# Chunk 0 of a two-layer kernel: heads 8 to 15 with the two batches of a pair exchanged on the partitions

## The chip, the cores and the metric

The kernel runs on one core of a Trainium2 chip. Its engines are TensorE (PE, matrix multiplications into the accumulator memory PSUM), VectorE (DVE), ScalarE (ACT), GpSimd (POOL) and SyncE (SP, which here issues transfers). Each engine executes its own instructions in order, and semaphores make one engine wait for another. The metric is the device time of one execution in microseconds: the median over several runs.

## The reference

Two layers, each a token mixer and a feed-forward block on the same normalised input. What the change touches is the second layer's mixer, a test-time-training layer with 16 heads of 64, working through each of 8 sequences of 256 tokens in 4 chunks of K = 64. Cut to the step that is looped over the chunks:

```
xq, xk, xv = hidden @ wq, hidden @ wk, hidden @ wv      # per head, per chunk
def step((W, b), (q, k, v)):
    eta  = token_eta * sigmoid(k @ theta + theta_bias) / HD
    Z1   = k @ W + b
    xhat = (Z1 - mean(Z1)) / std(Z1)
    go   = g * xhat + beta - (v - k)
    grad = (HD*go*g - sum(go*g) - xhat * sum(go*g*xhat)) / (HD * std)
    W    = W - einsum('bhkc,bhkd->bhcd', eta * k, grad)
    b    = b - sum over tokens (eta * grad)
    out  = q + g * normalise(q @ W + b) + beta
    return (W, b), out
```

W and b start the same for every sequence (W1 and b1). The first layer has a gated scan and a ternary feed-forward block with two gelu layers of 512 x 512; the second layer also has a mixture of 8 experts (two per token, chosen by `gate_w`) and a shared expert. All is float32.

## The kernel before, in words

**Tiles.** A tile of 128 partitions holds the 64 tokens of one chunk for two sequences: partitions 0 to 63 are the first batch of the pair, 64 to 127 the second. There are NCH = 4 chunks and NBP = 4 pairs, so the mixer has 16 units u, with chunk n = u // 4 and pair bp = u % 4. `xnT[n]` holds the normalised inputs of chunk n transposed (128 features on the partitions, 128 tokens of a pair along the row).

**One unit.** `keys` and `project_target` call `project` (L912), which multiplies the tokens of a pair with wk or wv: two matmuls, j = 0 for heads 0 to 7 and j = 1 for heads 8 to 15, each 128 tokens x 512, into two PSUM banks. ScalarE copies the keys to `xk`. `keys_T` transposes them (`pxkT`, L928), `apply_keys` multiplies by W (`pz`, L959), `states` adds the bias, `normalise` and `gradient` work out the gradient g on VectorE and GpSimd. `steps_of_W` then makes dW (`pw`, L1123) and the sums over tokens db (`pb`, L1130). `update` subtracts them (`W`, L1142; `B`, L1143), `apply_queries` multiplies the queries by the new W (`pzq`, L959), `outputs` adds B, and the rest normalises, transposes and mixes the heads (`poT`, `po`, L1184 and L1191).

**Quarters of the array.** `pw` and `pz` consist of 64 x 64 matmuls. The input partitions (0 to 63 or 64 to 127) and the output partitions fix which quarter of the 128 x 128 array a matmul uses, and the four orders of (a, b) in the loops use all four. `pb` is made by two full matmuls with `block_ones`, a 128 x 128 matrix with ones in its two diagonal blocks and zeros elsewhere: every batch's tokens are summed and written to all 64 partitions of that batch.

**The order.** Work of three units overlaps: in turn u, unit u computes its states, unit u - 1 its gradient and update, unit u - 2 its output. Between these, a `filler` issues pieces of other work: the first layer's feed-forward block of the following chunks (p, pm, po: L255 to L288), its residual and layernorm (L299, L186 to L202), the gates (L316), the routing, and later the experts. Up to the end of the first layer's scan all engines but GpSimd follow the order in which the program is written. In the mixer VectorE follows it, and TensorE and ScalarE are ordered by a planner.

**Gates.** `gates` (L316) multiplies each pair's tokens with `gw`, 24 columns: 8 for the experts' scores, 16 for the learning rate of each head, from which `eta` follows. The scores lead to the routing: with those of chunk 3 complete, VectorE makes `taken` (L667), SyncE reads values from it, and the experts' weights are fetched.

**PSUM.** Four single banks and two pairs of banks are rotated. `pk`, `pv`, `pxkT`, `pq`, `pz`, `pzq`, `pw`, `pb` and `poT` each take a pair, and wait until the one before it in that pair has been read.

Of the kernel before, what the change touches and what calls it, by code (L numbers as in the profile page):

```python
# [14 lines left out]
ALU = mybir.AluOpType  # L15
# [9 lines left out]
HH = H // 2  # L25
# [3 lines left out]
E = 8  # L29
# [27 lines left out]
C_EW2, C_EB1, C_EB2 = FF, 2 * FF, 2 * FF + 4  # L57
NEW = C_EB2 + D
I32 = mybir.dt.int32

# [11 lines left out]
def tile_two_layers(ctx: ExitStack, tc: tile.TileContext, t: dict, out: bass.AP):  # L74
    nc = tc.nc
# [10 lines left out]
    def bank(name):  # L86
        return ps1.tile([P, 512], F32, tag="bank", name=name)

    def two_banks(name):
        return ps2.tile([P, 2, 512], F32, tag="two", name=name)  # L90

    def resident(name, shape):
        return const.tile(shape, F32, tag=name, name=name)

    def resident_i(name, shape):
        return const.tile(shape, I32, tag=name, name=name)

    def load(name, shape, pool=const):
        sb = pool.tile(shape, F32, tag=name, name=name)
        nc.sync.dma_start(out=sb, in_=t[name])  # L100
        return sb
# [6 lines left out]
    block_ones = resident("block_ones", [P, P])  # L108
# [33 lines left out]
    xnT = [resident(f"xnT_{n}", [P, NBP, P]) for n in range(NCH)]  # L142
# [27 lines left out]
    def later(f):  # L170
        pending.append(f)
# [40 lines left out]
    def empty_rows(pool):  # L212
# [9 lines left out]
    nc.gpsimd.iota(  # L222
        second.bitcast(I32), [[P, NT]], base=B * S, channel_multiplier=1
    )
    nc.gpsimd.tensor_copy(second, second.bitcast(I32))
    wgt = resident("wgt", [P, NT, 2])
# [3 lines left out]
    gw = resident("gw", [P, E + H])  # L230
# [15 lines left out]
    def ffn_steps(n):  # L246

        s = {}
# [56 lines left out]
        def norm():  # L305
            s["row"] = const.tile([P, NBP, ROW], F32, tag="xn1", name="xn1")
            s["xn"] = s["row"][:, :, 0:D]
            ln_apply_T(x1[n], s["stats"], s["xn"], xnT[n])
            nc.gpsimd.tensor_copy(s["row"][:, :, D], second[:, mine])
            nc.gpsimd.tensor_tensor(x1[n], x1[n], kc[:, None, :].to_broadcast([P, NBP, D]), ALU.add)  # L310
            later(gates)

        def gates():
            s["pg"] = bank("pg")[:, : NBP * (E + H)].rearrange("p (b c) -> p b c", b=NBP)
            for bp in range(NBP):
                nc.tensor.matmul(s["pg"][:, bp, :], lhsT=xnT[n][:, bp, :], rhs=gw, start=True, stop=True)  # L316
            later(scores)

        def scores():
# [76 lines left out]
    with (  # L396
# [22 lines left out]
        wk = load("wk", [P, HC])  # L419
# [5 lines left out]
        wv = load("wv", [P, HC])  # L425
# [7 lines left out]
        hp = [l0b.tile([P, B, S + 3], F32, tag="hp", name="hp") for half in range(2)]  # L433
# [84 lines left out]
        for two in range(NBP // 2):  # L518

            pxp = bank("pxp").rearrange("p (b s) -> p b s", b=2)  # L520
            for half in range(2):
                for i in range(2):
                    b = 2 * (2 * two + i)
                    nc.tensor.matmul(
                        pxp[i * 64 : i * 64 + 64], lhsT=xp_w[:, half, :], rhs=hs[half][:, b : b + 2, :],
                        start=(half == 0), stop=(half == 1),
                    )
            part = xpT[:, 2 * two : 2 * two + 2, 0:S]
# [81 lines left out]
        for hp_ in range(HH):  # L610
            nc.tensor.matmul(
                pf2, lhsT=bpad[:, hp_, :], rhs=wo[:, hp_, :], start=(hp_ == 0), stop=(hp_ == HH - 1)
# [28 lines left out]
    def routing_steps():  # L641
        r = {}

        def work(name):

            return side["moe"].tile([P, NEW], F32, tag="ew", name=name, bufs=4)

        def constants():
            r["empty"] = empty_rows(side["moe"])
            w = r["w"] = work("rt_w")  # L650
            ints = w[:, 0:NJ].bitcast(I32)
            nc.gpsimd.iota(ints, [[1, NJ]], base=0, channel_multiplier=0)
# [123 lines left out]
    def routed_tokens_T(g):  # L776
        if g < NG:
            pt = bank("pxg")[:, : GJ * P].rearrange("p (j q) -> p j q", j=GJ)
            src = xg.pop(g)
            for j in range(GJ):  # L780
                nc.tensor.transpose(pt[:, j, :], src[:, j, 0:D], ident)
            ats[g] = side["moe"].tile([P, GJ], I32, tag="ats", name="ats", bufs=3)

# [109 lines left out]
    Wst = [l1.tile([P, 2, HH, HD], F32, tag=f"W_{bp}", name=f"W_{bp}") for bp in range(NBP)]  # L893
    Bst = [l1.tile([P, H, HD], F32, tag=f"B_{bp}", name=f"B_{bp}") for bp in range(NBP)]

    def heads(ap):
        return ap.rearrange("p (h d) -> p h d", h=H)
# [5 lines left out]
    def pairs_of(heads):  # L903
        return slice(heads.start // 2, heads.stop // 2)

    def full(ap):
        return ap.rearrange("p a b -> p (a b)")

    def project(xT, w, name):
        pp = two_banks(name)  # L910
        for j in range(2):
            nc.tensor.matmul(pp[:, j, :], lhsT=xT, rhs=w[:, j * 512 : (j + 1) * 512], start=True, stop=True)  # L912
        return heads(full(pp))

    def transpose_pairs(src, name, bufs=2, heads=ALL, held=None):
# [81 lines left out]
    class Unit:  # L997
# [10 lines left out]

        def keys(self):
            self.xk = l1b.tile([P, H, HD], F32, tag="xk", name="xk", bufs=3)  # L1010
            nc.scalar.copy(self.xk, project(xnT[self.n][:, self.bp, :], wk, "pk"))

        def keys_T(self):
            _, self.xkT = transpose_pairs(self.xk, "xkT", bufs=1)
# [4 lines left out]
                query_pairs(self.u // 2, HH // 2 * (self.u % 2))  # L1019

        def project_target(self):
            self.pv = project(xnT[self.n][:, self.bp, :], wv, "pv")

        def target(self):

# [77 lines left out]
        def steps_of_W(self, k=ALL):  # L1103
            if self.n == NCH - 1:

                part = pairs_of(k)
                for hp in range(part.start, part.stop):
                    for a in range(2):
                        for b in range(2):
                            rb = slice(b * 64, b * 64 + 64)  # L1110
                            nc.tensor.matmul(
                                self.z4[rb, a, hp, :], lhsT=self.at[rb, a, hp, :],
                                rhs=self.g[rb, 2 * hp + a, :], start=False, stop=(hp == HH - 1),
                            )
                return
            g = self.g
            self.pw = two_banks("pw")
            w4 = self.pw.rearrange("p b (h d) -> p b h d", h=HH)
            for hp in range(HH):
                for a in range(2):  # L1120
                    for b in range(2):
                        ra, rb = slice(a * 64, a * 64 + 64), slice(b * 64, b * 64 + 64)
                        nc.tensor.matmul(  # L1123
                            w4[ra, b, hp, :], lhsT=self.xk[rb, 2 * hp + a, :], rhs=g[rb, 2 * hp + a, :],
                            start=True, stop=True,
                        )
            self.w4 = w4
            self.pb = two_banks("pb")
            for j in range(2):
                nc.tensor.matmul(  # L1130
                    self.pb[:, j, :], lhsT=block_ones, rhs=full(g[:, j * HH : (j + 1) * HH, :]),
                    start=True, stop=True,
                )

        def update(self):

            if self.n == NCH - 1:
                return
            W, b = self.old()
            if self.n == 0:  # L1140
                W = W0[:, None].to_broadcast([P, 2, HH, HD])
            nc.vector.tensor_tensor(Wst[self.bp], W, self.w4, ALU.subtract)  # L1142
            nc.vector.tensor_tensor(Bst[self.bp], b, heads(full(self.pb)), ALU.subtract)  # L1143

        def apply_queries(self):
# [79 lines left out]
    for u in range(units - 1):  # L1225
# [3 lines left out]
        z, g, o = live.get(u), live.get(u - 1), live.pop(u - 2, None)  # L1229
# [76 lines left out]
    o, g, z = live[units - 3], live[units - 2], live[units - 1]  # L1306
# [202 lines left out]
```

## Time and profile before

| what | us |
|---|---|
| median of 9 runs | 582.08 (581.05 to 584.19) |
| the profiled execution | 583.11 |
| its span, first to last instruction | 581.4 |
| TensorE busy in the span | 534.7 |
| VectorE busy | 412.8 |
| pk, pv (L912), 64 records each | 31.8 each |
| pb (L1130), 48 records | 24.6 |
| pw (L1123), 768 records | 14.7 |
| pg (L316), 32 records | 5.0 |

A float32 matmul appears as two records in the profile. In a line such as `130.07 1.98 PE L1130 MATMUL pb<-gx,block_ones 128*128 128x512 f32 x4`, the numbers are the start and length in us, then come engine, line, operation, the tile written and the tiles read, the rows and columns of the array in use, the size moved, and the count of records. An idle time before it and what ended it follow in square brackets. In a table by stretch the columns are the stretch, its length, the busy time of TensorE's matmuls, its weight loads, VectorE, ScalarE and GpSimd, then the granted clock of TensorE, the share of the DMA engines and GB/s. The units of chunk 0 make their sums at about 130, 184, 233 and 262 us; their projections lie between 85 and 221 us.

### The profile page before, as it was taken

The page shows a single profiled execution, that of the slowest core. Times are in us where ns is not written, and L with a number is a line of the kernel's source. Part 1 is how long each engine was busy: PE and PEld are TensorE (multiplying, and loading weights), DVE is VectorE, ACT ScalarE, POOL GpSimd, SP SyncE. Part 2 cuts the span into 40 slices and gives each one's busy share as a digit, 9 for nine tenths or more (in the row PEclk, how much of TensorE's full clock was granted, in tenths as well). Part 3 has the DMA queues.
Part 4 walks back from the last instruction along what each step waited for, and adds up shares of the span by engine and source line. Part 5 has one row for each costly group of instructions (what it writes and reads, how often), then busy time and mean ns, then how long its engine had stood idle before and what let it go on. Part 6 is the DMA issues. An engine that isn't in the chain of part 4 may idle for free.

```text
span 581.4 us, 14158 instructions
## 1 busy us (share of the span) xinstructions
PE 534.7 (92%) x5887; PEld 369.9 (64%) x5887; DVE 412.8 (71%) x652; ACT 251.4 (43%) x436; POOL 289.0 (50%) x256
## 2 busy tenths in 40 slices
PE   5999999999999899998968899999999999999655
PEld 2443656465456546576755777888888887878644
DVE  4697353466650585757998598978888777878884
ACT  3655545316420443324505254553635546253246
POOL 6216103751651146542754456576755748467620
PEclk9999999999999799999989899999999999999888
DMA  7900200100000000000015425454353633100302
GB/s 282 406 12 25 61 1 6 33 1 2 12 14 13 1 9 15 17 0 2 19 53 167 141 93 172 135 191 146 108 174 118 203 116 125 43 16 6 109 20 89
DMA packets 25057, 45.89 MB, mean 79 GB/s; under 512 B 3860, under 2 KB 16026, under 8 KB 24481
## 3 DMA queue, kind: packets, MB, share of 16 engines
q1 hardware_dynamic: 22720, 40.75, 21.3%
q0 software_dynamic: 2272, 4.24, 2.2%
q8 instruction: 46, 0.75, 0.5%
q14 instruction: 19, 0.15, 0.1%
HBM read 38.30 MB, written 7.13 MB: 78 GB/s over the span
## 4 chain that ended last, share of the span: by engine, by line
PE 72%; DVE 12%; SPq 5%; issue 3%; ACT 3%; DMA 2%; POOL 2%; DVEq 0%; ACTq 0%; POOLq 0%
PE pm L271 19%; PE phd L804 5%; PE pv L912 4%; PE pyr L819 4%; PE pq L944 4%; PE pk L912 4%; PE po L1191 3%; PE pb L1130 3%; PE p L255 2%; PE po L282 2%; PE pz L959 2%; PE p L257 2%; PE pw L1123 2%; PE py L744 2%; DMA ew<-in_moe_w 2%
## 5 line engine op out<-in xcount | busy, mean ns | idle before, releaser
L271 PE MATMUL pm<-g,h 128*128 128x512 f32 x256 | 113.5, 595 | 0.0
L165 POOL TENSOR_TENSOR rstd<-rs_v,neg_half 128x16 f32<-128x16 f32 x31 | 92.2, 2973 | 2.6
L271 PEld LDWEIGHTS pm<-g,h 128*128 128x128 f32 x256 | 48.1, 190 | 59.8 <-issue 57.5
L1049 POOL TENSOR_TENSOR gx<-xh,gam 128x1024 f32<-128x1024 f32 (+1 forms) x17 | 38.3, 2252 | 81.7 <-DVE er L1048 56.1
L809 ACT ACTIVATE rhid<-phd,ew 128x128 f32<-128x128 f32 x156 | 44.6, 371 | 49.4 <-PE phd L804 38.1
L164 POOL TENSOR_SCALAR rs_v<-var 128x16 f32<-128x16 f32 x31 | 7.7, 247 | 93.4 <-DVE var L987 92.9
L275 ACT ACTIVATE g<-pm,cols 128x512 f32<-128x512 f32 x32 | 22.0, 687 | 68.3 <-PE pm L271 68.2
L804 PE MATMUL phd<-xgT,ew 128*128 128x128 f32 x312 | 43.9, 281 | 1.4 <-DMA ew<-in_moe_w 1.4
L153 POOL DMA_INDIRECT y_dram<-ys,ats x39 | 40.5, 1038 | 9.3 <-issue 9.3
L804 PEld LDWEIGHTS phd<-xgT,ew 128*128 128x128 f32 x312 | 39.4, 192 | 8.6 <-issue 5.1
L987 DVE TENSOR_REDUCE var<-sq 128x16 f32<-128x1024 f32 (+1 forms) x33 | 38.9, 1180 | 8.0 <-ACT sq L981 7.9
L819 PE MATMUL pyr<-ew,rhid 128*128 128x128 f32 x312 | 41.7, 275 | 0.0
L1027 DVE TENSOR_TENSOR u<-rows_b,pv 128x1024 f32<-128x1024 f32 x16 | 19.5, 1219 | 28.2 <-PE pv L912 28.1
L819 PEld LDWEIGHTS pyr<-ew,rhid 128*128 128x128 f32 x312 | 38.5, 192 | 1.5 <-issue 1.4
L1050 POOL TENSOR_TENSOR gx<-gx,u 128x1024 f32<-128x1024 f32 (+1 forms) x17 | 38.2, 2250 | 1.3
L153 POOL DMA_INDIRECT xg_dram<-xn,slot x32 | 34.4, 1076 | 8.3 <-issue 7.4
L981 ACT ACTIVATE sq<-o 128x1024 f32<-128x1024 f32 (+1 forms) x17 | 17.1, 1010 | 46.3 <-DVE o L970 46.3
L1191 PE MATMUL po<-wo,oT 128*128 128x128 f32 x256 | 33.0, 285 | 0.7 <-ACT oT L932 0.7
L912 PE MATMUL pk<-wk,xnT 128*128 128x512 f32 x64 | 31.8, 617 | 0.4 <-DVE o L970 0.4
L1191 PEld LDWEIGHTS po<-wo,oT 128*128 128x128 f32 x256 | 31.5, 201 | 1.0 <-ACT oT L932 0.9
L912 PE MATMUL pv<-wv,xnT 128*128 128x512 f32 x64 | 31.8, 617 | 0.0
L944 PE MATMUL pq<-xnT,wq 128*128 128x256 f32 x128 | 31.1, 383 | 0.4 <-DVE B L1143 0.4
(219 smaller groups left out, 1066.4 us busy)
## 6 DMA issues: line engine op xcount, KB each, us to landing
ew<-in_moe_w SPq DMA_DIRECT2D x39, 578.0 KB, 4.0
xg<-xg_dram SPq DMA_DIRECT2D x39, 65.0 KB, 3.2
h<-in_h SPq DMA_DIRECT2D x2, 1024.0 KB, 9.4
yc<-y_dram SPq DMA_DIRECT2D x8, 256.0 KB, 3.7
x<-in_x SPq DMA_DIRECT2D x4, 256.0 KB, 4.2
rows_g<-in_rows_g SPq DMA_DIRECT2D x1, 1024.0 KB, 7.7
rows_b<-in_rows_b SPq DMA_DIRECT2D x1, 1024.0 KB
w<-in_w SPq DMA_DIRECT2D x3, 256.0 KB, 3.9
```

What stands on the lines that cost most here:

```text
L153: ins = nc.gpsimd.indirect_dma_start(**what).ins
L165: turn[:] = [nc.gpsimd.tensor_tensor(dst, v[:, :width], neg_half[:, :width], ALU.pow).ins]
L271: nc.tensor.matmul(pm, lhsT=w[:, k, m * P : (m + 1) * P], rhs=s[src][:, k, :], start=(k == 0), stop=(k == 3),)
L804: nc.tensor.matmul(ph[:, ms], lhsT=w[:, ms], rhs=xgT[j // GJ][:, j % GJ, :], start=True, stop=True)
L809: nc.scalar.activation(hid[:, m, :], ph[:, ms], AF.Gelu, bias=w[:, C_EB1 + m : C_EB1 + m + 1])
L819: nc.tensor.matmul(py, lhsT=hid[:, m, :], rhs=w[:, C_EW2 + m * D : C_EW2 + (m + 1) * D], start=(m == 0), stop=(m == 3),)
L912: nc.tensor.matmul(pp[:, j, :], lhsT=xT, rhs=w[:, j * 512 : (j + 1) * 512], start=True, stop=True)
L944: nc.tensor.matmul(pq[:, i, :], lhsT=wq[:, (h0 + i) * P : (h0 + i + 1) * P], rhs=xnT[n][:, 2 * half : 2 * half + 2, :], start=True, stop=True,
L987: nc.vector.tensor_reduce(v[:, heads], sq[:, heads], AX.X, ALU.add)
L1049: nc.gpsimd.tensor_tensor(g, xh, gam2[:, k], ALU.mult)
L1050: turn[:] = [nc.gpsimd.tensor_tensor(g, g, self.t[:, k], ALU.add).ins]
L1191: nc.tensor.matmul(self.po, lhsT=self.oT[1][:, hp, :], rhs=wo[:, hp, :], start=False, stop=(hp == HH - 1),)
```

## The change

In chunk 0, heads 8 to 15 of all that is indexed by token have the second batch on partitions 0 to 63 and the first on 64 to 127. W and b are the same for every sequence at this point, so the work in between need not know of it. Three places make the exchange, two undo it:

- `project` with `turned`: the matmul of j = 1 becomes two of 64 columns, each taking the other batch's 64 tokens.
- `gates` for chunk 0: the learning rates of heads 8 to 15 are made in the same way, two matmuls of 64 output partitions and 8 columns, beside one full matmul of 16 columns per pair.
- `steps_of_W` leaves its sums to `sums`: in chunk 0, four matmuls of 64 x 64 on 512 columns take the place of the two with `block_ones` in full. For j = 0 they use the diagonal quarters, for j = 1 the other two, which puts the sums back to their own batch.
- `update` in chunk 0: dW of heads 8 to 15 lies in the other bank, so the subtraction is split into two instructions, the second reading the banks in reverse order.
- `pb` is allocated before the matmuls of `pw`, in all chunks but the last.

```diff
         def gates():
...
-                nc.tensor.matmul(s["pg"][:, bp, :], lhsT=xnT[n][:, bp, :], rhs=gw, start=True, stop=True)
+                xT, pg = xnT[n][:, bp, :], s["pg"][:, bp, :]
+                if n:
+                    nc.tensor.matmul(pg, lhsT=xT, rhs=gw, start=True, stop=True)
+                    continue
+                same = slice(0, E + HH)
+                nc.tensor.matmul(pg[:, same], lhsT=xT, rhs=gw[:, same], start=True, stop=True)
+                for b in range(2):
+                    nc.tensor.matmul(
+                        pg[b * 64 : b * 64 + 64, E + HH :], lhsT=xT[:, 64 - b * 64 : 128 - b * 64],
+                        rhs=gw[:, E + HH :], start=True, stop=True,
+                    )
...
+    def project(xT, w, name, turned=False):
...
+            if turned and j:
+                for b in range(2):
+                    nc.tensor.matmul(
+                        pp[b * 64 : b * 64 + 64, j, :], lhsT=xT[:, 64 - b * 64 : 128 - b * 64], rhs=wj,
+                        start=True, stop=True,
+                    )
+            else:
+                nc.tensor.matmul(pp[:, j, :], lhsT=xT, rhs=wj, start=True, stop=True)
...
+        def sums(self):
+
             for j in range(2):
-                nc.tensor.matmul(
-                    self.pb[:, j, :], lhsT=block_ones, rhs=full(g[:, j * HH : (j + 1) * HH, :]),
-                    start=True, stop=True,
-                )
+                gj = full(self.g[:, j * HH : (j + 1) * HH, :])
+                if self.n:
+                    nc.tensor.matmul(self.pb[:, j, :], lhsT=block_ones, rhs=gj, start=True, stop=True)
+                    continue
+                for b in range(2):
+                    rb, to = slice(b * 64, b * 64 + 64), b if j == 0 else 1 - b
+                    nc.tensor.matmul(
+                        self.pb[to * 64 : to * 64 + 64, j, :], lhsT=block_ones[rb, rb], rhs=gj[rb],
+                        start=True, stop=True,
+                    )
...
-            nc.vector.tensor_tensor(Wst[self.bp], W, self.w4, ALU.subtract)
+                for part, w4 in ((slice(0, HH // 2), self.w4), (slice(HH // 2, HH), self.w4[:, ::-1])):
+                    nc.vector.tensor_tensor(Wst[self.bp][:, :, part], W[:, :, part], w4[:, :, part], ALU.subtract)
+            else:
+                nc.vector.tensor_tensor(Wst[self.bp], W, self.w4, ALU.subtract)
```

`project` is called with `turned` set to `self.n == 0` for the keys and for the targets; the queries are not turned.

More of the change, by code (lines that the diff above doesn't have):

```diff
@@ L907, in full @@
         return ap.rearrange("p a b -> p (a b)")
-    def project(xT, w, name):
+    def project(xT, w, name, turned=False):
         pp = two_banks(name)
         for j in range(2):
-            nc.tensor.matmul(pp[:, j, :], lhsT=xT, rhs=w[:, j * 512 : (j + 1) * 512], start=True, stop=True)
+            wj = w[:, j * 512 : (j + 1) * 512]
+            if turned and j:
[6 more added lines that the diff above has]
+                nc.tensor.matmul(pp[:, j, :], lhsT=xT, rhs=wj, start=True, stop=True)
         return heads(full(pp))
@@ L1010, in keys @@
             self.xk = l1b.tile([P, H, HD], F32, tag="xk", name="xk", bufs=3)
-            nc.scalar.copy(self.xk, project(xnT[self.n][:, self.bp, :], wk, "pk"))
+            nc.scalar.copy(self.xk, project(xnT[self.n][:, self.bp, :], wk, "pk", self.n == 0))
         def keys_T(self):
@@ L1021, in project_target @@
         def project_target(self):
-            self.pv = project(xnT[self.n][:, self.bp, :], wv, "pv")
+            self.pv = project(xnT[self.n][:, self.bp, :], wv, "pv", self.n == 0)
         def target(self):
@@ L1116, in steps_of_W @@
             g = self.g
-            self.pw = two_banks("pw")
-            w4 = self.pw.rearrange("p b (h d) -> p b h d", h=HH)
+            self.pw, self.pb = two_banks("pw"), two_banks("pb")
+            self.w4 = self.pw.rearrange("p b (h d) -> p b h d", h=HH)
             for hp in range(HH):
@@ L1123, in steps_of_W @@
                         nc.tensor.matmul(
-                            w4[ra, b, hp, :], lhsT=self.xk[rb, 2 * hp + a, :], rhs=g[rb, 2 * hp + a, :],
+                            self.w4[ra, b, hp, :],
+                            lhsT=self.xk[rb, 2 * hp + a, :], rhs=g[rb, 2 * hp + a, :],
                             start=True, stop=True,
                         )
-            self.w4 = w4
-            self.pb = two_banks("pb")
+            self.sums()
+        def sums(self):
             for j in range(2):
-                nc.tensor.matmul(
-                    self.pb[:, j, :], lhsT=block_ones, rhs=full(g[:, j * HH : (j + 1) * HH, :]),
-                    start=True, stop=True,
-                )
+                gj = full(self.g[:, j * HH : (j + 1) * HH, :])
[8 more added lines that the diff above has]
+                    )
         def update(self):
```

## The prediction

> **What bounds the kernel now.** I read the page's busy shares first, then the sums by stretch over the time in which chunk 0 is handled.
>
> ```profile
> PE 534.7 (92%) x5887; PEld 369.9 (64%) x5887; DVE 412.8 (71%) x652; ACT 251.4 (43%) x436; POOL 289.0 (50%) x256
> ```
> ```profile
> 74.00:129.00 55.00, 54.99 (x341) 30.20 (x339) 24.69 (x46) 20.84 (x25) 25.00 (x18) 1.00 0.03 11
> 129.00:192.00 63.00, 60.83 (x478) 33.46 (x481) 32.76 (x72) 22.24 (x26) 23.57 (x20) 1.00 0.03 10
> ```
> TensorE (PE, the second number) is busy for 54.99 of the first 55 us and 60.83 of the next 63; VectorE (DVE, fourth) for about half. So in the stretch that the change touches, a TensorE microsecond is a microsecond of the end, except beside the few waits. The chain of work that ended last shows the price of each form. Its columns are start, length, piece; every f32 matmul is two records.
>
> ```profile
> 52.04 3.58 PE pxp L524 x16
> 55.63 3.64 PE pm L271 x8
> ...
> 75.11 0.81 PE pg L316 x8
> ...
> 104.88 1.72 PE pk L912 x4
> ...
> 136.69 1.00 PE pg L316 x8
> ...
> 142.31 1.95 PE pk L912 x4
> ```
> Full-array matmuls of 512 columns in a row take 1.72 / 4 = 0.43 us a record (pk at 104.88). L524 is the form that the change introduces: 64 output columns, 512 moving, two halves of the array. Its 16 records take 3.58 us, so they run two at a time: 8 steps x 0.43 = 3.44, and 0.14 is left over. The full-array pm behind it takes 3.64 for 8 records instead of 8 x 0.43 = 3.44: 0.20 more. Likewise pk at 142.31, after 64x64 matmuls, takes 1.95 instead of 1.72, and pg at 136.69 1.00 instead of 0.81. So **a change of tiling costs TensorE time in both directions**: 0.14 us going into tiles, 0.20 coming back, 0.34 for a visit. Every price below comes from this.
>
> **The change part by part.**
>
> *Projections (keys and values of the four chunk 0 units, 8 calls).* The second half, one full matmul of 2 x 0.43 = 0.86, becomes two of 64 columns. By L524 the two run together in 0.86, so the streaming is unchanged, but a visit to tiles is added. In the instruction order of the changed kernel, seven of the eight go full, two tiled, full: 7 x 0.34 = 2.4 us. The eighth, the keys of unit 3, comes out differently, because the planner orders TensorE here: its two halves are pulled apart, with pn, p and four pm matmuls between them. Neither has a partner: 0.86 more streaming and two visits, 0.86 + 0.68 = 1.5 us. ScalarE's copy of these keys moves behind one gelu; it is hidden by the eight pm matmuls (8 x 0.86 us) that still stand ahead of the transposes reading it. Sum +3.9.
>
> *Gates (L316 of chunk 0).* Four matmuls (0.81 us) become four with 16 columns and eight with 8 columns on half the array, alternating. The narrow full ones cost what the wide ones did, 0.2 us each: at 24 columns, the time isn't in the columns. The trace has no 8-column tile; the nearest is pw, 64 records in 1.16 us below, sixteen groups of four at about 0.06. Two such steps four times are 0.5; four visits at 0.34 are 1.4. Sum 1.9; since pg's own return cost (1.00 against 0.81) includes a first weight load that was preloaded in the other case, the three inner returns may be some 0.06 cheaper: I take +1.7, between 1.5 and 1.9. TensorE does not wait between 73.66 and 132 us, so all of it counts.
>
> *Sums over tokens (L1130, pb).* Two full matmuls, 4 x 0.43 = 1.72, become four on the four quarters. Whether four run at once is told by pw; whether two with different input rows can write one bank, by L1111:
>
> ```profile
> 128.97 1.16 PE L1123 MATMUL pw<-gx,xk 64*64 64x64 f32 x64
> 130.07 1.98 PE L1130 MATMUL pb<-gx,block_ones 128*128 128x512 f32 x4
> 132.78 1.10 PE L201 MATMUL ln_pt<-ident,xn 128*128 128x128 f32 x4 [0.73 <-DVE xn L198]
> ```
> ```profile
> 502.26 2.08 PE L1111 MATMUL pzq<-gx,rows_b 64*64 64x64 f32 x64 [1.08 <-DVE gx L1065]
> ```
> 64 records in 1.16 us on four quarters, 2.08 on two: four really work at once, and the two diagonal quarters of L1111, which share a bank, work at once too. So pb should take two steps, 0.86, with no change of tiling between pw and pb; the return moves behind pb. TensorE saves 0.86 per unit, and a whole visit more where tiled matmuls follow. The bounds are 0.86 (all four together), 1.72 (in pairs) and 3.44 (one by one); I take 0.86, as pw and L1111 cover both halves of the pattern. The Trainium skill, "TensorEngine Tiling (Array Packing)", Gotcha 1, says that different row tiles can't access one PSUM bank at the same time. By that, pb would go in pairs at best and save nothing; L1111's 2.08 us, twice pw's for half the quarters, speaks against it: in turns it would be about four times pw's.
>
> What of it reaches the end differs by unit. Unit 0: pb is followed by ln_pt, which waits 0.73 us for DVE's xn, set by the layernorm of po, which was ready before pw: nothing. Unit 1 (184.05): the po matmuls that the next layernorm needs stand behind pb: -0.86. Unit 2 is set by DVE:
>
> ```profile
> 233.17 1.22 DVE L1142 TENSOR_TENSOR W<-W,pw 128x1024 f32<-128x1024 f32 x1 [0.83 <-PE pw L1123]
> 235.06 1.22 DVE L1143 TENSOR_TENSOR B<-rows_b,pb 128x1024 f32<-128x1024 f32 x1 [0.67 <-PE pb L1130]
> 236.38 1.23 DVE L970 TENSOR_TENSOR o<-pzq,B 128x1024 f32<-128x1024 f32 x1
> ```
> B waits 0.67 us for pb, and pz waits for B to free pb's banks. With pb early, B starts as soon as W lets it: the gain is those 0.67 less W's lengthening, and its next limit, pzq behind W, lies at the same place: -0.6. Unit 3: pb ends beside the next layernorm, before ln_pt at 265.22, which waits 0.94 us: nothing. Sum -1.5.
>
> *Update of W (L1142).* One instruction of 1024 becomes two of 512. A 512-wide tensor_tensor from PSUM (L299) takes 0.69 against 1.22, so two are 0.16 longer apart from overlap; consecutive ones overlap by 0.09 (W to B at 190.44 and 191.54). Between 0 and 0.16: I take 0.08. It is on the path at unit 1 (xn waits behind W and B on DVE) and unit 3 (pzq waits for W): +0.2. At unit 0 it is covered by the p matmuls ahead of pzq. No wait is added and SP's and GpSimd's orders are unchanged, as is DVE's but for the split.
>
> **Sum:** 3.9 + 1.7 - 1.5 + 0.2 = +4.3 us. The rest carries it: the routing that starts the experts hangs on DVE's `taken` at 293.14, which stands on DVE behind the residual at 292.94 that waits for TensorE's output mix. The profiled execution took 583.11 (span 581.4 and 1.7 around it), 1.0 over the median of the runs shown; its own sum gives 587.4. The median, 582.08, gives 586.4, which I forecast.
>
> One thing moves by itself, the granted clock:
>
> ```profile
> 191.77 1.16 PE L959 MATMUL pzq<-W,xqT 64*64 64x64 f32 x64 [1.45 <-DVE W L1142]
> 193.75:200.60 6.85, 6.85 (x35) 4.36 (x35) 0.95 (x3) 3.79 (x5) 1.27 (x1) 0.50 0.01 2
> ```
> After the wait of 1.45 us for W the clock is 0.50 for 6.85 us, which loses 3.4. The wait remains, W's split making it slightly longer, so I expect the halving in most runs of both kernels. The Trainium skill, "TensorE: Matmul & The Clock Gate", Part 1, puts the return to half clock after at least one idle window of about 3.4 us; by that no halving would belong here, and 1.45 us of idling shows otherwise. The nine runs spread over 3.1 us, and I give the gate 2 us on either side.
>
> **Rivals.**
> *Pairs in the sums:* quarters that share a bank take turns, pb stays at 1.72, and the 1.5 gained is lost: 587.9. For: no row has four 512-column tiles at once. Against: L1111. Chance 0.09. One by one, 3.44, costs 1.7 more than before at units 1 and 2 and shows by some 0.8 at the other two, despite their waits: 4.3 + 1.5 + 3.4 + 1.6 = 10.8, 592.9. Chance 0.04.
> *Not felt, or no price for changing tiles:* if the experts' start did not hang on TensorE, the 5.1 us in which TensorE waits before 301.03 would swallow everything: 582.1. If the visits to the new 64-column tiles were free, thirteen of them (9 projections' and 4 of the gates') would give back 13 x 0.34 = 4.4: 582.0. Against the first speaks the order on DVE, against the second L524's own 0.14 and 0.20. Chances 0.04 and 0.03.
> *Faster, through the clock:* the halving after 191.77 vanishes, because the shifted work puts that wait across the border of whatever the gate measures (3.4 us), and the one around 300 us goes with it (clock 0.85 on average over 293 to 316, 23 x 0.15 = 3.4 us, two thirds of it with TensorE busy: 2.3). That is 5.7: 586.4 - 5.7 = 580.7. It decides from 5.5 us on. For: a 1.45 us wait is a narrow cause. Against: the spread of 3.1 over nine runs suggests that no phase gives so much. Chance 0.05.
>
> **How the numbers follow.** The forecast, slower by 4.3 with 2 for the gate and 0.4 for the unknown terms, has 0.75: 584.2 to 588.6, which takes in the pairs case too and leaves out the rest, so the range is the same. Faster than 0.2% (1.2 us, about what a measurement tells from no change) 0.05, within it 0.07, slower 0.75 + 0.09 + 0.04 = 0.88.
>
> **What would show it.** In the changed profile: pb at 0.86 to 0.9 us for eight records right behind pw, else the pairs; the chunk 0 pk and pv pieces with their pm behind at 0.34 more than before, and unit 3's pk split around pm; pg of chunk 0 with its return at 2.5 us instead of 0.81; B of unit 2 directly behind W. By the start of `taken` the delay should be about 4.3 us. The forecast is wrong if that delay is there and the end doesn't have it, or if a visit to 64-column tiles costs well under 0.34.

## The result, and the profile after

The changed kernel takes 590.09 us (median of 10; 587.3 to 594.2) against 581.67 (median of 31 runs of the kernel before): 1.0146 of it, 95% interval 1.0126 to 1.0165. That is 8.4 us slower. The forecast was slower by 4.3, 584.2 to 588.6: the sign was right, the size half of what came. The profiled execution took 590.24, its span is 588.5, 7.1 over the span of before.

The page's busy times and the granted clock in 40 slices:

```profile
PE 539.9 (92%) x5935; PEld 368.8 (63%) x5935; DVE 412.9 (70%) x656; ACT 251.5 (43%) x436; POOL 289.4 (49%) x256
...
PEclk9999999998999999996998899999999999999878
```

TensorE has 48 more matmul records and 5.2 us more busy time. The clock row has a dip in the tenth slice that the kernel before doesn't have, and the deep one that it had in the fourteenth is gone and stands in the nineteenth. So two things are to be told apart: the work that was added, and the clock.

**The work.** The chain of waits of the changed kernel, where the gates and the first keys are made (start, length, piece):

```profile
75.54 0.13 PE pg L323 x2
75.67 0.22 PE pg L325 x4
75.89 0.32 PE pg L323 x2
76.21 0.22 PE pg L325 x4
...
77.52 1.06 PE p L257 x2
78.57 0.86 PE p L259 x2
79.43 6.87 PE pm L273 x16
...
86.66 0.94 PE pk L932 x2
87.60 1.01 PE pk L927 x4
88.61 1.92 PE pm L273 x4
```

The gates' four full pieces (L323) and four tiled ones (L325) end at 77.52, and p behind them takes 1.06 instead of 0.95; from the first pg to the first p the timelines give 2.07 us against 0.81 before, 1.26 more. The turned half of pk takes 1.01 for two pairs of records (2 x 0.43 + 0.15) and the pm behind it 1.92 instead of 1.72: a visit is 0.35. Set side by side start by start, the two timelines drift apart by 0.35 at each of the seven ordinary projections (the drift is how much later the same piece starts in the changed kernel). At unit 3's keys the halves stand apart:

```profile
148.33 1.00 PE pk L927 x2
...
151.69 3.43 PE pm L273 x8
155.13 1.00 PE pk L927 x2
156.13 7.06 PE pm L273 x16
```

Two records each, 1.00 us each, alone: the drift grows by 1.54 here, visits included. The sums and the update, unit 2 (VectorE):

```profile
237.21 1.29 DVE L1172 TENSOR_TENSOR W<-W,pw 128x512 f32<-128x512 f32 x2 [0.83 <-PE pw L1143]
238.41 1.22 DVE L1175 TENSOR_TENSOR B<-rows_b,pb 128x1024 f32<-128x1024 f32 x1
```

B follows W without the wait of 0.67. The drift falls by 0.69 here and by 0.86 behind unit 1's pb.

**The clock.** TensorE around unit 0's sums and unit 3's, in the changed kernel's timeline:

```profile
133.38 1.04 PE L1159 MATMUL pb<-gx,block_ones 64*64 64x512 f32 x8
136.20 1.25 PE L203 MATMUL ln_pt<-ident,xn 128*128 128x128 f32 x4 [1.78 <-DVE xn L200]
137.24 1.92 PE L257 MATMUL p<-xnT,w 128*128 128x512 f32 x2
...
265.55 1.04 PE L1159 MATMUL pb<-gx,block_ones 64*64 64x512 f32 x8
268.59 1.10 PE L203 MATMUL ln_pt<-ident,xn 128*128 128x128 f32 x4 [2.00 <-DVE xn L200]
270.65 1.99 PE L979 MATMUL pzq<-W,xqT 64*64 64x64 f32 x64 [0.95 <-DVE W L1172]
272.56 1.90 PE L320 MATMUL pg<-gw,xnT 128*128 128x24 f32 x8
```

Eight records of pb in 1.04 us (0.86 and the last one's tail): the four quarters do work at once. But the layernorm decides when ln_pt starts, so the time saved is added to a wait: 1.78 us instead of 0.73 at unit 0, 2.00 and 0.95 instead of 0.94 and 0.80 at unit 3. Behind these waits, p, pzq and pg take up to twice their time. The table by stretch shows why (the clock is the third number from the right):

```profile
133.25:136.66 3.41, 1.63 (x33) 0.56 (x22) 1.99 (x12) 0.00 (x0) 1.22 (x2) 1.00 0.02 5
136.66:140.07 3.41, 3.41 (x7) 1.47 (x6) 2.57 (x4) 2.56 (x3) 1.28 (x1) 0.50 0.00 0
194.69:198.10 3.41, 1.90 (x23) 0.71 (x24) 3.38 (x12) 1.97 (x2) 1.24 (x2) 1.00 0.00 0
266.37:269.78 3.41, 1.32 (x8) 0.56 (x4) 1.97 (x10) 0.05 (x1) 1.74 (x4) 1.00 0.00 0
269.78:280.02 10.24, 9.37 (x145) 7.98 (x145) 5.59 (x18) 6.01 (x9) 0.88 (x1) 0.50 0.01 2
```

The clock changes on a grid of 3.41 us. Where TensorE was busy for only 1.63 or 1.32 us of a cell, the next one or three cells run at half clock; behind the cell with 1.90, none does. The same waits in the kernel before, on its own grid:

```profile
132.31:135.72 3.41, 2.94 (x20) 1.35 (x23) 3.34 (x6) 1.78 (x2) 1.32 (x2) 1.00 0.00 0
262.00:265.42 3.42, 2.48 (x31) 1.04 (x21) 1.95 (x12) 0.00 (x0) 2.26 (x9) 1.00 0.02 5
265.42:268.83 3.41, 2.61 (x74) 2.07 (x73) 2.77 (x4) 1.87 (x2) 1.27 (x1) 1.00 0.00 0
```

Busy for 2.48 us or more, and no halving. In the drift of this pair of executions the half clock costs 1.5 us at 137 and 3.8 at 270; against that, the halving that before has at 193.75 is missing (2.9), of which a wait of pk at 209 takes 0.6 back. With the 3.9 us of the terms, and 0.4 by which the changed kernel is later already ahead of the gates, where nothing was changed, that makes 7.3 at the start of unit 4's pw. Nothing is added behind it: the spans differ by 7.1.

### The profile page after: what moved, and what is told of

It is laid out like the page before. It is cut to its first block, busy times and chain, and to the rows that moved or that the text cites. A ratio compares the mean times of both kernels' runs of the same rounds, so it can differ in the third digit from the quotient of the medians.

```text
span 588.5 us, 14262 instructions
## 1 busy us (share of the span) xinstructions
PE 539.9 (92%) x5935; PEld 368.8 (63%) x5935; DVE 412.9 (70%) x656; ACT 251.5 (43%) x436; POOL 289.4 (49%) x256
## 4 chain that ended last, share of the span: by engine, by line
PE 72%; DVE 17%; ACT 3%; POOL 2%; issue 2%; DMA 2%; SPq 1%; DVEq 0%; ACTq 0%; POOLq 0%
PE pm L273 19%; PE phd L816 5%; PE pq L964 4%; PE pyr L831 4%; PE pk L932 3%; PE pv L932 3%; PE po L1223 3%; PE pb L1155 3%; PE p L257 3%; PE pm L741 2%; PE po L284 2%; PE pz L979 2%; PE p L259 2%; DMA ew<-in_moe_w 2%; PE pzq L979 2%
## 5 line engine op out<-in xcount | busy, mean ns | idle before, releaser
L979 PE MATMUL pzq<-W,xqT 64*64 64x64 f32 x1024 | 20.5, 233 | 10.4 <-DVE W L1174 5.1
L979 PEld LDWEIGHTS pzq<-W,xqT 64*64 64x64 f32 x1024 | 18.1, 145 | 18.2 <-DVE W L1174 9.0
```

The source lines that it names most:

```text
L979: ins = nc.tensor.matmul(z4[rb, a, hp, :], lhsT=xT[ra, hp, t0 + b * 64 : t0 + b * 64 + 64], rhs=W[ra, hp, :] if W is W0 else W[ra, b, hp, ...
```

## The experiments

The theory then: the terms of the sum are about right (3.9 by the drifts), and the rest is the clock, halved because the saving lengthens waits. The rival: the saving is worth what it is, and the clock is chance. The experiments ran on three other chips (e1 to e4 on one, e5 to e8 on the next, e9 and e10 on the third), where the kernel before takes 594.5 to 594.8 us, so each ratio is to that kernel's runs on the same chip. Beside the ratio I give the **time at half clock**, 2 x (1 - mean granted clock) x span, averaged over the compared executions. In these traces the clock is either 1.0 or 0.5, so it says how long TensorE ran at half. These averages have standard errors of 0.9 to 3.6 us, the largest for e5 with its six executions.

| run | ratio to before (95%) | half clock, us (before beside it) |
|---|---|---|
| e1_full_sums | 1.0080 (1.0053 to 1.0107) | 31.8 (31.8) |
| e2_sums_twice | 1.0099 (1.0063 to 1.0136) | 35.0 (31.8) |
| e3_quarters_0_3 | 1.0043 (1.0009 to 1.0078) | 39.6 (31.8) |
| e4_quarters_1_2 | 0.9990 (0.9958 to 1.0021) | 31.3 (31.8) |
| e5_changed_again | 1.0131 (1.0085 to 1.0178) | 35.6 (29.6) |
| e6_before_filled | 1.0002 (0.9973 to 1.0031) | 29.0 (29.6) |
| e7_changed_filled | 1.0060 (1.0038 to 1.0082) | 28.6 (29.6) |
| e8_turned_copy | 1.0024 (0.9998 to 1.0050) | 28.9 (29.6) |
| e9_tail_filled | 1.0016 (0.9990 to 1.0042) | 25.3 (29.0) |
| e10_quarters_twice | 1.0007 (0.9976 to 1.0037) | 28.8 (29.0) |

### Less work, beside a wait: e3 and e10

```diff
 # e3: the kernel before, steps_of_W
             for j in range(2):
...
+                gj = full(g[:, j * HH : (j + 1) * HH, :])
+                if self.u not in (0, 3):
+                    nc.tensor.matmul(self.pb[:, j, :], lhsT=block_ones, rhs=gj, start=True, stop=True)
+                    continue
+                for b in range(2):
+                    rb, to = slice(b * 64, b * 64 + 64), b if j == 0 else 1 - b
+                    nc.tensor.matmul(
+                        self.pb[to * 64 : to * 64 + 64, j, :], lhsT=block_ones[rb, rb], rhs=gj[rb],
+                        start=True, stop=True,
+                    )
 # e10: the same, and around it
+            for again in range(2 if self.u in (0, 3) else 1):
```

> The kernel before, with the sums on four quarters at units 0 and 3 alone and nothing exchanged (the sums of heads 8 to 15 then land at the other batch: that step is left out). TensorE has 0.86 us less to do in each, beside a wait. Clock theory: the waits grow to 1.8 and 2.0 us, the clock halves behind them in most runs, and less work makes the kernel slower by about 3.4 us: 1.006 (1.003 to 1.009). Rival, my costing at nothing: 1.000.

> The kernel before with the sums of units 0 and 3 on four quarters, as in the run with the quarters at units 0 and 3, but made twice, so that TensorE works as long there as before (the sums of heads 8 to 15 land at the other batch: that step is left out). Clock theory: waits as before, 1.000 (0.998 to 1.002), and a mean clock like before's. Rival, it is the quarters themselves or the change of tiling behind them that made that run slower: 1.004 again.

e3 is 1.0043 (2.6 us slower), e10 1.0007. Nothing differs between the two kernels but how often the same matmuls are made. The timeline of e3:

```profile
131.14 1.04 PE L1136 MATMUL pb<-gx,block_ones 64*64 64x512 f32 x8
133.97 1.10 PE L201 MATMUL ln_pt<-ident,xn 128*128 128x128 f32 x4 [1.79 <-DVE xn L198]
134.91 1.05 PE L255 MATMUL p<-xnT,w 128*128 128x512 f32 x2
135.77 1.90 PE L257 MATMUL p<-xnT,w 128*128 128x512 f32 x2
...
271.45 1.90 PE L316 MATMUL pg<-gw,xnT 128*128 128x24 f32 x8
273.18 3.76 PE L729 MATMUL pm<-xnT,shared_w 128*128 128x256 f32 x8
```

and of e10:

```profile
131.61 1.90 PE L1137 MATMUL pb<-gx,block_ones 64*64 64x512 f32 x16
134.43 1.10 PE L201 MATMUL ln_pt<-ident,xn 128*128 128x128 f32 x4 [0.93 <-DVE xn L198]
135.37 1.02 PE L255 MATMUL p<-xnT,w 128*128 128x512 f32 x2
136.23 1.02 PE L257 MATMUL p<-xnT,w 128*128 128x512 f32 x2
...
269.68 1.07 PE L316 MATMUL pg<-gw,xnT 128*128 128x24 f32 x8
270.60 1.97 PE L729 MATMUL pm<-xnT,shared_w 128*128 128x256 f32 x8
```

With 0.86 us more work in pb, p takes 1.02 instead of 1.90 and pm 1.97 instead of 3.76. Averaged over executions, e3 has 7.8 us more at half clock than before, which at half speed loses up to 3.9; 2.6 were measured. e10 has as much half clock as before. By the times alone the test is close: e3's interval leaves out the 1.000 of its rival and e10's the 1.004 of its own, both narrowly, and the two intervals, from two chips, overlap. With the half clock and the timelines beside them, both rivals fall: time saved beside a wait was paid back with interest.

### The saving where it is on the chain: e4

> The kernel before, with the sums on four quarters at units 1 and 2 alone, nothing exchanged (the sums of heads 8 to 15 land at the other batch). There the saving is on the chain: 0.86 and 0.69 us. Both theories: 1.55 us faster, 0.9973, since no wait grows by it but the short one at unit 2 (0.64 us). If the quarters cost something elsewhere: 1.000 or more.

0.9990 with an interval that holds both 0.9973 and 1.000: the gain of 1.55 us isn't shown by the time, nor excluded.

### The change without its saving, and with the waits filled: e1, e2, e5, e7

```diff
 # e1: the changed kernel, sums by two full matmuls in chunk 0 too
-                if self.n:
+                if True:
 # e2 and e7: the sums of units 0 and 3 made twice
             self.sums()
+            if self.u in (0, 3):
+                self.sums()
 # e6 and e7: one matmul of no use ahead of pzq at units 1 and 3
+BEFORE_PZQ = {1: 1, 3: 1}
...
+                keep_busy(BEFORE_PZQ.get(self.u, 0))
```

> The changed kernel with the sums over tokens of chunk 0 again by two full matmuls (the exchange of heads 8 to 15 is then not undone in the sums: that step of the result is left out). Clock theory: what the change saves beside a wait of TensorE lengthens that wait past what the clock gate bears (1.78 us at unit 0, 2.0 and 0.95 at unit 3), and the halvings that follow cost more than the saving. Without the saving those waits are 0.7 and 0.9 again: 1.55 us are lost at units 1 and 2, about 3.4 regained from the clock, so the time is about 2 us below the changed kernel, 1.011 of before (1.008 to 1.014). Rival, the change's terms are as the trace shows and the clock is chance: 1.55 us above the changed kernel, 1.017 of before.

> The changed kernel, whose four matmuls of the sums are made twice at units 0 and 3, with the same result: 0.86 us more work for TensorE in each. Clock theory: the waits behind them shrink to about 0.9 and 1.1 us, the halvings at 137 and 270 us go, and more work makes the kernel faster by about 3.4 us: 1.0086 of before (1.006 to 1.011). Rival, the clock is chance: no faster than the changed kernel, 1.0145 of before or a little more.

> The changed kernel itself once more, beside the next three on one chip: 1.0145 of before (1.0126 to 1.0165) by the first measurement. Both theories the same; it is the base of the others.

> The changed kernel with the same two matmuls and with the sums of units 0 and 3 made twice. Clock theory: no halving is left between 120 and 290 us, and what remains of the change is the sum of its own terms, 3.9 us over the filled kernel before (gates 1.25, visits to tiles and the split keys 4.0, sums -1.55, W 0.2): 1.004 of before, 0.0067 over the filled kernel before. Rival: still 1.0145, or 0.014 over it.

The change again costs 1.0131 (7.8 us), with 6.0 us more at half clock than before. Its six executions fall into two groups: two took 596.99 and 597.30 us at a mean clock of 0.981 and 0.978, the other four 602.19 to 604.45 at 0.965 to 0.967. So the same kernel takes about 6 us less where the mean clock is higher. With the waits filled (e7) it costs 1.0060 (3.6 us) and has no more half clock than before: about the terms alone, as expected. Its interval ends at 1.0082, far below the rival's 1.0145 and just below e5's lower end, 1.0085.

Without its saving (e1) the change is at 1.0080, the low end of what was expected, with exactly before's half clock. That is 4.8 us, where the terms less the saving make 5.4: taking the saving out made the changed kernel no slower. e2 is between (1.0099, 3.2 us more at half clock). It left 1.5 us at unit 1 and the second wait at unit 3, which e7 filled; that these make the difference is argued, not shown, and the one halving that e2's profiled execution has before 300 us speaks for another place. It comes at 240.08, behind unit 2's pzq:

```profile
237.44 0.36 PE L979 MATMUL pzq<-W,xqT 64*64 64x64 f32 x6 [0.38 <-issue]
238.20 0.34 PE L979 MATMUL pzq<-W,xqT 64*64 64x64 f32 x4 [0.40 <-issue]
238.91 0.35 PE L979 MATMUL pzq<-W,xqT 64*64 64x64 f32 x5 [0.36 <-issue]
```

All ten profiled executions of the experiments, of both kernels, have such gaps in or right behind this pzq, in which the profile shows nothing that TensorE waits for; the two of the first chip have none. e2, e4, e7 and e9 halve right behind them. They are no part of the change, but they add to the noise, and in e5 and e8 the saving at unit 2 mostly goes into them.

There is a direct reading of the terms, too. The profiled execution of e5, the one of 597.30 us, has no halving in the stretch from chunk 0's gates to the start of unit 4's pw, nor has that of e6:

```profile
75.23:297.32 222.09, 212.55 (x1787) 121.99 (x1785) 129.72 (x249) 81.91 (x104) 95.05 (x77) 1.00 0.03 10
```
```profile
75.78:294.58 218.80, 213.35 (x1743) 126.07 (x1741) 129.51 (x245) 82.03 (x104) 95.26 (x77) 1.00 0.03 10
```

The clock is 1.00 in both and the stretch 3.3 us longer (222.09 against 218.80), a little under e7's 3.6 and the 3.9 of the drifts. It is no exact measure: e6 loses 1.2 us at 102, with gaps inside a pz that e5 doesn't have, and of the 0.69 saved at unit 2 only 0.15 comes through here.

The same execution sets a limit to the theory. Its waits at units 0 and 3 are those of the first profile (1.78, 2.00 and 0.95 us), and the cells around them were busy for little more:

```profile
132.78:136.19 3.41, 1.62 (x53) 0.73 (x44) 1.95 (x12) 0.00 (x0) 1.22 (x2) 1.00 0.02 5
265.90:269.31 3.41, 1.65 (x64) 0.77 (x54) 1.94 (x11) 0.00 (x0) 2.70 (x9) 1.00 0.00 0
```

No halving followed. And e1's profiled execution does halve at 271.96, behind waits of only 0.94 and 0.95 us. So the longer waits make a halving likelier, not certain; where the grid falls on a wait differs between executions.

### Filling the waits of the kernel before: e6 and e9

`keep_busy(k)` issues k full 128x512 matmuls into a free bank; e9 calls it ahead of four waits after 535 us.

> The kernel before with one full 128x512 matmul (0.86 us, its result unused) in each of two waits of TensorE, ahead of pzq of units 1 and 3. Clock theory: the waits of 1.45 and of 0.94 + 0.80 us fall to 0.6 and 0.9, so none of the halvings between 120 and 290 us is left; before has them in a part of its executions only, so 1 to 2 us faster: 0.9975 (0.995 to 1.000). Rival, the clock is chance: 1.000 or a little more.

> The kernel before with full 128x512 matmuls, their results unused, in four waits of TensorE after 535 us: three ahead of unit 14's last matmuls on W (a wait of 3.26 us), two ahead of the first half of unit 15's (2.84), one ahead of unit 14's poT (1.71) and one ahead of unit 15's (1.93). Clock theory: the waits fall to 0.7 to 1.1 us, the halvings at 542, 556 and 566 us (3.4 us each) go; where TensorE sets the end there, up to half of 10.2 us comes back, but the chain there is mostly VectorE and ScalarE, so 1 to 2 us: 0.9975 (0.994 to 1.000). Rival, the halvings there cost nothing: 1.000.

Both missed: 1.0002 and 1.0016. e6 leaves the half clock where it was, so before seldom loses it there. e9 takes 3.7 us of half clock away (its profiled execution still has three halvings of one cell each between 550 and 590 us) and gains nothing: in the chain of before after 535 us most pieces are VectorE's and ScalarE's. That a halving costs only where TensorE bounds is argued from this.

### The exchange without the visits: e8

e8 is e7 with the projections changed as below, and with the four full matmuls of the gates ahead of the eight narrow ones.

```diff
+    turnedT = ...    # a view of the W tile of pair 3, not written before unit 3's update
+    for b in range(2):
+        nc.gpsimd.tensor_copy(
+            turnedT[:, :, b * 64 : b * 64 + 64], xnT[0][:, :, 64 - b * 64 : 128 - b * 64]
+        )
...
+            lhsT = turned if turned is not None and j else xT
+            nc.tensor.matmul(pp[:, j, :], lhsT=lhsT, rhs=wj, start=True, stop=True)
```

> The filled changed kernel, with the exchange made without visits to tiles: GpSimd copies the chunk 0 inputs with the two batches' columns exchanged (into memory of W that isn't used yet), the second half of each projection is one full matmul on that copy, and the gates make their four full matmuls first and then the eight narrow ones, one visit in all. By the terms: gates 0.7, visits 0, sums -1.55, W 0.2, so 0.6 us under the filled kernel before, 0.9965 of before. If the visits are not what the projections cost: as the filled changed kernel.

In the same stretch its profiled execution takes 218.92 us at full clock, 3.2 less than e5. Beside e6's it drifts by less than 0.1 us at each of the eight projections, so the visits and the split keys are what the projections cost. Over e6's 218.80 there is no gain, where 0.6 was expected: the saving at unit 2 is lost in the gaps of its pzq. The whole is 1.0024, not told from before. No version tried here is shown to beat the kernel before.

## Why the prediction was wrong

- **What bounds, and the price of a visit: right.** 0.35 was measured where 0.34 was worked out, at seven projections, and the split keys of unit 3 cost 1.54 against 1.5. The delay at the start of unit 4 also reaches the end, as the prediction had it.
- **Gates: somewhat too dear.** +1.26 against +1.7 (1.5 to 1.9). An inner return costs about 0.12 there (0.32 for two records against a quarter of 0.81), where 512-column matmuls paid 0.20; why is not shown.
- **Sums: right.** Eight records in 0.86 and a tail, -0.86 and -0.69 on the chain. The rival of turns in pairs is out. The Trainium skill, "TensorEngine Tiling (Array Packing)", Gotcha 1, has row tiles unable to use one bank at the same time; here two with different input rows and different output partitions did, at full speed, and the measurement decides.
- **Update of W: right** (+0.06 at unit 1 and +0.16 at unit 3, against 0.2 in all).
- **The sum of terms: 3.3 to 3.9 measured, 4.3 forecast.**
- **The step that failed: "Unit 0 ... nothing" and "Unit 3 ... nothing".** I costed the saving there at zero, because a wait hid it, though the same prediction shows a wait of 1.45 us followed by half clock. With the gate I went wrong in the same way: "I expect the halving in most runs of both kernels", with 2 us on either side as if it were noise common to both. Of the nine profiled executions that leave unit 1's wait unfilled, only two halve behind it (before and e4). What came was in the main the change's own effect: the waits at units 0 and 3 grew from 0.73 and 0.94 us to 1.78 and 2.00, and the clock then halves behind them in many executions, though not in all (in the first profile and in e3's, not in e5's). e3 shows it without the exchange (2.6 us); filling the waits takes 4.2 us off the change (7.8 to 3.6).
- **The faster rival** named the right mechanism with the wrong sign: the halving near 193 us did go in this one execution, but two others came.

Open: the 4 us of the clock aren't split between units 0, 1 and 3, how often the longer waits halve the clock is known from few executions, and e2's remainder isn't settled.

## What to carry to other kernels

Time saved on TensorE beside a wait is not free: add it to the wait, and ask whether the wait then passes half a cell of the clock's grid, and whether TensorE bounds what follows. Count the changes of tiling before packing the array; a pair of half-array matmuls gains nothing over one full matmul, and every visit here cost 0.35 us against 0.86 saved by four quarters. In a compiled order, look whether tiles that are to run together still stand together.

## What the runs showed of the hardware

The gate does not ask for a whole idle cell. Over the twelve profiled executions here, cells of 3.41 us at full clock in which TensorE idled for less than 30% were followed by half clock 1 time in 1747, 30 to 50% 12 times in 104, 50 to 60% 13 in 16, and over 60% 47 in 47. The Trainium skill, "TensorE: Matmul & The Clock Gate", Part 1, puts the threshold at one idle window of about 3.4 us; the grid agrees, the threshold doesn't. A halving lasts one to three cells, also where TensorE is busy all through (136.66 to 140.07). And work that nobody needs can be free, as far as these intervals tell: e10's doubled sums are not told from before in time, while leaving them short (e3) cost 2.6 us.
